# Products of quarters that accumulate in three PSUM banks, in place of seven banks added up by VectorE

## The chip, the cores and the metric

One core of a Trainium2 chip runs the whole program. The metric is the device time of one execution in microseconds; the time of a kernel is the median of its runs. TensorE multiplies and writes PSUM (eight banks); VectorE, ScalarE and GpSimd do the elementwise work, GpSimd on SBUF alone; SyncE issues the DMAs. In the profile they are PE (its weight loads are PEld), DVE, ACT, POOL and SP.

## The reference

64 graphs of 256 nodes with 512 features go through two layers, each on a normalised input (`h = relu(layernorm(x))`) and added to `x`. All values are float32.

```python
# layer 0: graph attention, one head
Wh = h @ W
logits = leaky_relu(Wh @ a_src [rows] + Wh @ a_dst [columns], 0.2)
x = x + softmax(where(adj, logits, -inf)) @ Wh
# layer 1: multi-head attention, 8 heads of 64
q, k, v = h @ Wq.T + bq, h @ Wk.T + bk, h @ Wv.T + bv
scores = where(adj, q @ k.T / sqrt(64), -inf)
x = x + (softmax(scores) @ v) @ Wo.T + bo
```

## The kernel before

**Products of quarters.** A product of a 256 x 512 and a 512 x 512 matrix is taken in quarters: each factor is split two by two, and seven products of quarters (of sums and differences of quarters) replace eight. GpSimd makes the four sums of the left factor (`combine`, L163 to L168), in the order s[0], s[1], s[2], s[3]; the weights' sums are made once. Product 0 uses the left quarter a(0,0), 1 uses s[1], 2 uses a(0,1), 3 uses s[2], 4 uses s[0], 5 uses a(1,1) and 6 uses s[3]. `products` (L170) gives each its own PSUM bank from a pool of eight, and after each product calls `read`, which adds the bank to the quarters of the result that it belongs to.

Four product sets of this kind run per graph. W, in `transform0`, adds the first layer's result to the rows of x; O, in `output`, the second layer's. Both read with `add_to_rows` (L723), one VectorE instruction for each product that adds the bank to as many as four quarters of x at once (`TARGETS`). K, in `project_qk`, makes q and k together (eight matmuls of 128 columns per product, `product_cols`), and V, in `project_v`, makes v. These two read with `add_up` (L190), in which VectorE forms intermediate sums; ScalarE reads product 0 and, in K, copies product 4 with a bias into `p5` for VectorE. A fifth set, U in `aggregate0`, also uses `products` and `add_up`; each of its products has two matmuls.

**The pass.** The program is unrolled in Python, and each engine executes its own queue in the order in which the program issues. That order is written out by hand in two lists: `first_half` (L1072) and `second_half` (L1075). One pass through both handles several graphs at different stages. Each letter runs its stage up to the next `yield`, so each K, V, W or O is one product with its read. In `first_half` the products of O (graph i-2) and K (graph i) alternate; between the first O and the first K stands D0, whose VectorE part is four dot products of 128 x 512 (L526). AS_OLD issues the sums `as` of O's left factor on GpSimd after the first K. O takes its products in the order 0, 2, 5, 1, 3, 4, 6, the other sets in the order 0 to 6. The exponentials of E0 (L557, L558) wait on ScalarE for a DMA.

In `second_half` come A (attention: scores in all eight banks, exponentials on ScalarE, masks on VectorE), the seven W, and among them the first V, then N1, the statistics of the next graph: N1 (`normalize1`, L738) is a mean and a sum of squares on ScalarE for one half of the rows, then, one step later, for the other half, then the normalised rows `xn`. After these come the other six products of V, with A's masks, U, and X1. X1 (`transpose1`, L766) transposes `xn` in two steps; ScalarE writes the result into `hT` (L779), of which there is one buffer, and its third step issues the sums `hs` on GpSimd, also one buffer. `hT` and `hs` are the left factor of the next K and V. The end of the list is X1, V, X1, V, X1, and then the next pass begins with O and K.

Of the kernel before, what the change touches and what calls it, by code (L numbers as in the profile page):

```python
# [9 lines left out]
F32 = mybir.dt.float32  # L10
I32 = mybir.dt.int32
AF = mybir.ActivationFunctionType
# [4 lines left out]
P = 128  # L17
# [11 lines left out]
def kernel(  # L29
# [102 lines left out]
    def bounded():  # L132
# [37 lines left out]
        def products(a, s, name, product, read, order=range(7)):  # L170


            plan = (
                (a(0, 0), B11),
                (s[:, 1], T2),
                (a(0, 1), B21),
                (s[:, 2], T3),
                (s[:, 0], T1),
                (a(1, 1), T4N),
                (s[:, 3], B22),  # L180
            )
            for n in order:
                left, slot = plan[n]
                ps = bank([P, D], f"{name}_{n}")
                product(ps, left, slot)
                read(n, ps)
                yield

        def add_up(n, ps, dst, s2):

            if n == 1:
                nc.vector.tensor_add(s2, dst(0, 0), ps)
            elif n == 2:
                nc.vector.tensor_add(dst(0, 0), dst(0, 0), ps)  # L194
            elif n == 3:
                nc.vector.tensor_add(dst(1, 0), s2, ps)
            elif n == 4:
                nc.vector.tensor_add(dst(1, 1), dst(1, 0), ps)
                nc.vector.tensor_add(dst(0, 1), s2, ps)
            elif n == 5:  # L200
                nc.vector.tensor_add(dst(1, 0), dst(1, 0), ps)
            elif n == 6:
                nc.vector.tensor_add(dst(0, 1), dst(0, 1), ps)

        def product_rows(wt, dst, left, slot):
            for c in range(2):
                nc.tensor.matmul(  # L207
                    dst[:, 0:HD], left[:, c, :], wt[:, slot, c, :], start=c == 0, stop=c == 1
                )

        def product_cols(wts, dst, left, slot):
            for n, wt in enumerate(wts):
                for e in range(2):
                    at = (2 * n + e) * P
                    for c in range(2):
                        nc.tensor.matmul(  # L216
                            dst[:, at : at + P], wt[:, slot, c, e * P : (e + 1) * P], left[:, c, :],
                            start=c == 0, stop=c == 1,
                        )

        xts = {}
# [81 lines left out]

        bias0 = weights.tile([P, 4], F32, tag="bias0", name="bias0")
        bias10 = weights.tile([P, 4], F32, tag="bias10", name="bias10")

        def prepare_biases():
            for n, col in enumerate((cols["bq"], cols["bk"])):  # L310
                nc.vector.tensor_copy(bias0[:, 2 * n : 2 * n + 2], col[:, 0:2])
                nc.vector.tensor_sub(bias10[:, 2 * n : 2 * n + 2], col[:, 2:4], col[:, 0:2])

        def whole(wt):

# [362 lines left out]
        def layer0(g):  # L678
# [37 lines left out]
                if m == 0:  # L716
                    yield

        TARGETS = (
            (0, 4, 1), (1, 4, 1), (0, 1, 1), (2, 4, 1), (1, 4, 2), (2, 3, 1), (1, 2, 1)  # L720
        )

        def add_to_rows(xt, n, ps):  # L723

            quarters = xt.rearrange("p t (j d) -> p (t j) d", j=2)
            first, end, step = TARGETS[n]
            dst = quarters[:, first:end:step, :]
            src = ps[:, 0:HD].unsqueeze(1).to_broadcast([P, dst.shape[1], HD])
            nc.vector.tensor_add(dst, src, dst)  # L729

        def transform0(g):

            a, s = sums0.pop(g)
            yield from products(
                a, s, f"po0_{g}", partial(product_rows, w_sb), partial(add_to_rows, xts[g])
            )

        def normalize1(g):  # L738
            xt = xts[g]

            first = 1 if g else 0
            if g:
                xn = junk = big.tile([P, NT, D], F32, tag="xn", name=f"xn_{g}")
            else:
                junk = work.tile([P, NT, D], F32, tag="ex", name="junk_1", bufs=4)
            stats = Stats(xt, junk, f"1_{g}")
            stats.mean(first)
            stats.squares(first)
            yield
            stats.mean(1 - first)  # L750
            stats.squares(1 - first)
            nmr, rstd = stats.close()
            yield
            if g == 0:
                xn = big.tile([P, NT, D], F32, tag="xn", name=f"xn_{g}")
            for t in range(NT):
                nc.scalar.activation(
                    xn[:, t, :], xt[:, t, :], AF.Identity,
                    bias=nmr[:, t : t + 1], scale=rstd[:, t : t + 1],
                )  # L760
            norms[g] = xn
            yield
# [22 lines left out]
        def project_qk(g):  # L785
            halves = [
                big.tile([P, 4, TOK], F32, tag=f"qk{j}", name=f"qk{j}_{g}")
                for j in range(2)
            ]
            qkv[g] = halves  # L790
            if g == 0:

                for e in range(DC):
                    for n, (wt, nm) in enumerate(((wq_sb, "bq"), (wk_sb, "bk"))):
                        ps = bank([P, TOK], f"pqk_{g}_{e}_{n}")
                        for c in range(DC):
                            part = whole(wt)[c // 2][e // 2][:, c % 2, :]
                            nc.tensor.matmul(
                                ps, part[:, (e % 2) * P : (e % 2 + 1) * P], hT_0[0][:, c, :],
                                start=(c == 0), stop=(c == DC - 1),  # L800
                            )
                        nc.scalar.activation(
                            halves[e // 2][:, 2 * n + e % 2, :], ps, AF.Identity,
                            bias=cols[nm][:, e : e + 1],
                        )
                        yield
                return
            a, s = lefts[g]

            s2 = work.tile([P, 4, P], F32, tag="s2", name=f"s2_{g}")  # L810
            held = []

            def dst(i, j):
                return halves[j][:, :, i * P : (i + 1) * P]

            def read(n, ps):
                ps = ps.rearrange("p (c n) -> p c n", c=4)
                if n == 0:
                    for c in range(4):
                        nc.scalar.activation(  # L820
                            dst(0, 0)[:, c, :], ps[:, c, :], AF.Identity, bias=bias0[:, c : c + 1]
                        )
                elif n == 4:
                    p5 = work.tile([P, 4, P], F32, tag="p5", name=f"p5_{g}")
                    for c in range(4):
                        nc.scalar.activation(
                            p5[:, c, :], ps[:, c, :], AF.Identity, bias=bias10[:, c : c + 1]
                        )
                    held.append(p5)
                    return  # L830
                if held:
                    add_up(4, held.pop(), dst, s2)
                add_up(n, ps, dst, s2)

            yield from products(a, s, f"pqk_{g}", partial(product_cols, (wq_sb, wk_sb)), read)

        def project_v(g):
            a, s = lefts.pop(g)
            v = [big.tile([P, NT, HD], F32, tag=f"v{j}", name=f"v{j}_{g}") for j in range(2)]
            s2 = work.tile([P, HD], F32, tag="s2v", name=f"s2v_{g}")  # L840
            vs[g] = v

            def dst(i, j):
                return v[j][:, i, :]

            def read(n, ps):
                if n == 0:
                    nc.scalar.copy(dst(0, 0), ps[:, 0:HD])
                add_up(n, ps[:, 0:HD], dst, s2)

            yield from products(a, s, f"pv_{g}", partial(product_rows, wv_sb), read)

        def attention(g):

# [137 lines left out]
        def output(g):  # L992
            xt = xts.pop(g)
            a, s = outs.pop(g)
            def store(t):
                row = (g * NT + t) * P
                nc.sync.dma_start(out_rows[row : row + P, :], xt[:, t, :])

            def read(n, ps):
                add_to_rows(xt, n, ps)  # L1000
                if n in (4, 6):
                    store(1 if n == 4 else 0)

            if g < G - 2:

                yield from products(
                    a, s, f"po1_{g}", partial(product_rows, wo_sb), read, (0, 2, 5, 1, 3, 4, 6)
                )
                return

            for t in range(NT):
# [325 lines left out]
```

## Time and profile before

| what | us |
|---|---|
| median of three runs (2813.95 to 2815.35) | 2814.04 |
| span of the profiled execution | 2812.4 |
| one pass of the loop (from one W product to the same one of the next pass) | 43.2 |
| VectorE: add_to_rows (L729), 875 reads | 594.6 |
| VectorE: masks of the attention (L879), 512 | 368.3 |
| VectorE: dot products (L526), 252 | 276.3 |
| VectorE: sums of K from SBUF (L198, L199), 63 each | 84.8 and 75.8 |
| ScalarE: K's product 0 (L820) and product 4 (L826), 252 each | 71.8 and 70.1 |
| ScalarE: exponentials of the attention (L874), 512 | 257.8 |
| GpSimd: longest wait, for a DMA (L606) | 454.1 |

The span is the time from the first to the last instruction of one profiled execution. "Busy" is the time in which an engine had an instruction running; matmuls overlap, so a group's busy time is less than its count times its mean. A matmul of float32 appears as two records. "Idle before" is the time that an engine stood ahead of a group, with the instruction that ended it. GpSimd's and ScalarE's long waits are not by themselves a cost: what counts is who is late for TensorE.

### The profile page before, as it was taken

How to read it: one execution, taken by the hardware profiler on the slowest of the kernel's cores; microseconds unless marked ns; L12 is line 12 of the kernel's file. 1: busy time of each engine (PE TensorE's matmuls, PEld its weight loads, DVE VectorE, ACT ScalarE, POOL GpSimd, SP SyncE). 2: the span in 40 equal slices, each digit the busy share in tenths (PEclk: the TensorE clock that was granted, in tenths of full speed). 3: DMA queues.
4: the chain of work that ended last, by engine and by line, in shares of the span. 5: the costliest groups of instructions: out<-in, count | busy, mean ns of one | idle time of the engine just before them, and what ended most of it. 6: DMA issues, size and time to landing. Idle time of an engine off the chain costs nothing. (4 is left out here: it accounts for less than half of the span.)

```text
span 2812.4 us, 54529 instructions
## 1 busy us (share of the span) xinstructions
PE 2797.5 (99%) x20560; PEld 2462.1 (88%) x20560; DVE 2333.9 (83%) x3942; ACT 1255.3 (45%) x3033; POOL 1505.3 (54%) x2020
## 2 busy tenths in 40 slices
PE   9999999999999999999999999999999999999999
PEld 6888988988889889888898898888988988889886
DVE  7888888888888888888888888888888888888875
ACT  6354453443544444534444445344444453444532
POOL 2745555555555555555555554555555645555541
PEclk9999999999999999999999999999999999999999
DMA  4233343343333434433434344334343443343331
GB/s 135 29 44 41 41 52 37 44 49 40 44 42 41 52 38 44 51 37 44 43 40 52 39 44 52 37 44 44 42 48 39 43 52 37 44 44 42 40 45 28
DMA packets 144321, 127.15 MB, mean 45 GB/s; under 512 B 65204, under 2 KB 110132, under 8 KB 144054
## 3 DMA queue, kind: packets, MB, share of 16 engines
q1 hardware_dynamic: 143958, 123.61, 36.8%
q8 instruction: 165, 2.70, 0.4%
q14 instruction: 102, 0.84, 0.1%
q0 software_dynamic: 96, 0.01, 0.0%
HBM read 41.43 MB, written 33.55 MB: 27 GB/s over the span
## 5 line engine op out<-in xcount | busy, mean ns | idle before, releaser
L729 DVE TENSOR_TENSOR x<-po,x 128x1024 f32<-128x1024 f32 x875 | 594.6, 686 | 149.0 <-PE po L207 141.8
L879 DVE TENSOR_TENSOR ex<-ex,maskT 128x512 f32<-128x512 f32 x512 | 368.3, 760 | 0.0
L606 POOL TENSOR_TENSOR em<-em,rb 128x256 f32<-128x256 f32 x122 | 86.3, 728 | 454.1 <-DMA rb<-rc 454.1
L874 ACT ACTIVATE ex<-psc 128x512 f32<-128x512 f32 x512 | 257.8, 627 | 99.7 <-PE psc L866 99.7
L526 DVE SCALAR_TENSOR_TENSOR junk<-wa,h 128x512 f32<-128x512 f32 x252 | 276.3, 1096 | 7.6 <-ACT h L519 0.9
L216 PEld LDWEIGHTS pqk<-hs,wq_sb 128*128 128x128 f32 x2016 | 264.3, 192 | 13.5 <-POOL hs L166 0.7
L216 PE MATMUL pqk<-hs,wq_sb 128*128 128x128 f32 x2016 | 265.9, 275 | 0.5 <-POOL hs L166 0.5
L216 PE MATMUL pqk<-hs,wk_sb 128*128 128x128 f32 x2016 | 266.3, 275 | 0.0
L557 ACT ACTIVATE e<-es_b,ed 128x256 f32<-128x256 f32 x122 | 61.0, 500 | 445.0 <-DMA es_b<-es_row 445.0
L207 PE MATMUL po<-wo_sb,as 128*128 128x256 f32 x992 | 255.2, 380 | 0.0
L207 PE MATMUL pv<-wv_sb,hs 128*128 128x256 f32 x1024 | 252.6, 379 | 0.5 <-DVE v L194 0.5
L207 PE MATMUL po<-w_sb,us 128*128 128x256 f32 x1008 | 248.4, 379 | 0.0
L216 PEld LDWEIGHTS pqk<-hs,wk_sb 128*128 128x128 f32 x2016 | 245.4, 192 | 0.0
L866 PE MATMUL psc<-qk 64*128 64x256 f32 x2048 | 240.0, 384 | 0.0
L891 PE MATMUL pav<-ex,v 128*64 128x256 f32 x2048 | 237.0, 382 | 1.2 <-DVE ex L879 1.2
L565 POOL TENSOR_TENSOR em<-e,maskT 128x512 f32<-128x512 f32 x62 | 79.6, 1284 | 266.8 <-DVE e L562 257.1
L165 POOL TENSOR_TENSOR hs<-hT 128x256 f32<-128x256 f32 x64 | 47.3, 738 | 320.9 <-PE pv L207 320.9
L866 PEld LDWEIGHTS psc<-qk 64*128 64x128 f32 x2048 | 194.0, 188 | 27.1 <-ACT aT L899 0.8
L207 PEld LDWEIGHTS po<-w_sb,us 128*128 128x128 f32 x1008 | 191.5, 190 | 26.0
L207 PEld LDWEIGHTS pv<-wv_sb,hs 128*128 128x128 f32 x1024 | 189.6, 190 | 24.0 <-DVE v L194 0.9
L899 ACT COPY aT<-pav 128x512 f32<-128x512 f32 x128 | 74.9, 585 | 297.8 <-PE pav L891 130.8
L891 PEld LDWEIGHTS pav<-ex,v 128*64 128x64 f32 x2048 | 141.3, 137 | 75.7 <-DVE ex L879 2.5
(218 smaller groups left out, 6403.5 us busy)
## 6 DMA issues: line engine op xcount, KB each, us to landing
x<-in_x_dram SPq DMA_DIRECT2D x64, 512.0 KB, 5.6
out_dram<-x SPq DMA_DIRECT2D x128, 256.0 KB, 2.0
rb<-rc SPq DMA_DIRECT2D x496, 64.0 KB, 5.1
es_b<-es_row SPq DMA_DIRECT2D x61, 128.0 KB, 6.4
rb<-rc SPq DMA_DIRECT2D x244, 32.0 KB, 3.8
es_row<-es SPq DMA_DIRECT2D x122, 0.5 KB, 1.9
wq_sb<-in_L_gnn_Wq_dram SPq DMA_DIRECT2D x4, 256.0 KB, 8.1
wk_sb<-in_L_gnn_Wk_dram SPq DMA_DIRECT2D x4, 256.0 KB, 6.7
```

The lines of the kernel that those rows point to most:

```text
L207: nc.tensor.matmul(dst[:, 0:HD], left[:, c, :], wt[:, slot, c, :], start=c == 0, stop=c == 1)
L216: nc.tensor.matmul(dst[:, at : at + P], wt[:, slot, c, e * P : (e + 1) * P], left[:, c, :], start=c == 0, stop=c == 1,)
L526: nc.vector.scalar_tensor_tensor(junk, (wa if g else pas)[a], 1.0, h[:, t, :], op0=ALU.mult, op1=ALU.mult, accum_out=dst[:, t : t + 1],)
L557: nc.scalar.activation(e1[:, m, :], pe, AF.Exp, bias=ed[:, m : m + 1])
L565: engine.tensor_tensor(em, e1, maskT, op=ALU.mult)
L606: nc.gpsimd.tensor_tensor(em[:, m, :], em[:, m, :], rb, op=ALU.mult)
L729: nc.vector.tensor_add(dst, src, dst)
L866: nc.tensor.matmul(psc[r][:, m, :], qk[rows, 2 + e % 2, m * P : (m + 1) * P], qk[rows, e % 2, :], start=True, stop=True,)
L874: nc.scalar.activation(ex[:, r, :, :], psc[r], AF.Exp, scale=SCALE)
L879: nc.vector.tensor_mul(ex[:, r, :, :], ex[:, r, :, :], maskT)
L891: nc.tensor.matmul(pav[r * DH : (r + 1) * DH, i, :], v[j][:, m, at : at + DH], pair[i][:, r, m, :], start=(m == 0), stop=(m == NC - 1),)
L899: nc.scalar.copy(aT[j], pav)
```

## The change

W, O, K and V use `chained` in place of `products`. The products run in the order 0, 2, 1, 4, 3, 6, 5 in three banks: 0, 1, 3 and 5 in bank `a`, 2 in `b`, 4 and 6 in `d`. Only the first product in a bank starts it anew; the later ones add to what stands in it. The bank is read after each product, before the next one is written on top, so each read gives one quarter of the result, or one addend of it, and the intermediate sums of VectorE fall away. O loses its own order. ScalarE now copies products 0, 1, 4 and 5 in K (with a bias, four instructions each) and in V (one each); VectorE adds 2, 3 and 6. In W and O VectorE reads every product and adds it to one quarter. `normalize1` takes the rows' first half first, and `output` stores the second half of the rows after product 5 and the first after product 6. U stays as it was.

```diff
+        CHAIN = ((0, "a"), (2, "b"), (1, "a"), (4, "d"), (3, "a"), (6, "d"), (5, "a"))
+        def chained(a, s, name, product, read):
...
+            banks = {}
+            for n, key in CHAIN:
+                left, slot = plan[n]
+                first = key not in banks
+                if first:
+                    banks[key] = bank([P, D], f"{name}_{key}")
+                product(banks[key], left, slot, first)
+                read(n, banks[key])
+                yield
+        def assemble(n, ps, dst, copy):
+            if n == 0:
+                copy(dst(0, 0), ps, 0)
+            elif n == 2:
+                nc.vector.tensor_add(dst(0, 0), dst(0, 0), ps)
+            elif n == 1:
+                copy(dst(0, 1), ps, 1)
+            elif n == 4:
+                copy(dst(1, 1), ps, 1)
+            elif n == 3:
+                nc.vector.tensor_add(dst(1, 1), dst(1, 1), ps)
+            elif n == 6:
+                nc.vector.tensor_add(dst(0, 1), dst(0, 1), ps)
+            elif n == 5:
+                copy(dst(1, 0), ps, 0)
...
-                    dst[:, 0:HD], left[:, c, :], wt[:, slot, c, :], start=c == 0, stop=c == 1
+                    dst[:, 0:HD], left[:, c, :], wt[:, slot, c, :],
+                    start=first and c == 0, stop=c == 1, skip_group_check=not first,
...
-                            start=c == 0, stop=c == 1,
+                            start=first and at == 0 and c == 0, stop=c == 1,
+                            skip_group_check=True,
...
-        bias0 = weights.tile([P, 4], F32, tag="bias0", name="bias0")
-        bias10 = weights.tile([P, 4], F32, tag="bias10", name="bias10")
+        biases = [weights.tile([P, 4], F32, tag=f"bias{j}", name=f"bias{j}") for j in range(2)]
...
-        TARGETS = (
-            (0, 4, 1), (1, 4, 1), (0, 1, 1), (2, 4, 1), (1, 4, 2), (2, 3, 1), (1, 2, 1)
-        )
+        TARGETS = ((0, 0), (0, 1), (0, 0), (1, 1), (1, 1), (1, 0), (0, 1))
...
-            nc.vector.tensor_add(dst, src, dst)
+            t, j = TARGETS[n]
+            part = xt[:, t, j * HD : (j + 1) * HD]
+            nc.vector.tensor_add(part, ps[:, 0:HD], part)
...
-            yield from products(
+            yield from chained(
                 a, s, f"po0_{g}", partial(product_rows, w_sb), partial(add_to_rows, xts[g])
...
-            first = 1 if g else 0
+            first = 0
...
+            def copy(to, ps, j):
+                for c in range(4):
+                    nc.scalar.activation(
+                        to[:, c, :], ps[:, c, :], AF.Identity, bias=biases[j][:, c : c + 1]
+                    )
...
-            yield from products(a, s, f"pqk_{g}", partial(product_cols, (wq_sb, wk_sb)), read)
+                assemble(n, ps.rearrange("p (c n) -> p c n", c=4), dst, copy)
+            yield from chained(a, s, f"pqk_{g}", partial(product_cols, (wq_sb, wk_sb)), read)
...
+            def copy(to, ps, j):
+                nc.scalar.copy(to, ps)
...
-            yield from products(a, s, f"pv_{g}", partial(product_rows, wv_sb), read)
+                assemble(n, ps[:, 0:HD], dst, copy)
+            yield from chained(a, s, f"pv_{g}", partial(product_rows, wv_sb), read)
...
-                if n in (4, 6):
-                    store(1 if n == 4 else 0)
+                if n in (5, 6):
+                    store(1 if n == 5 else 0)
...
-                yield from products(
-                    a, s, f"po1_{g}", partial(product_rows, wo_sb), read, (0, 2, 5, 1, 3, 4, 6)
-                )
+                yield from chained(a, s, f"po1_{g}", partial(product_rows, wo_sb), read)
```

More of the change, by code (lines that the diff above doesn't have):

```diff
@@ L187, in products @@
                 yield
+        CHAIN = ((0, "a"), (2, "b"), (1, "a"), (4, "d"), (3, "a"), (6, "d"), (5, "a"))
+        def chained(a, s, name, product, read):
+            plan = (
+                (a(0, 0), B11),
+                (s[:, 1], T2),
+                (a(0, 1), B21),
+                (s[:, 2], T3),
+                (s[:, 0], T1),
+                (a(1, 1), T4N),
+                (s[:, 3], B22),
+            )
[23 more added lines that the diff above has]
+                copy(dst(1, 0), ps, 0)
         def add_up(n, ps, dst, s2):
@@ L203, in add_up, with product_rows, product_cols @@
                 nc.vector.tensor_add(dst(0, 1), dst(0, 1), ps)
-        def product_rows(wt, dst, left, slot):
+        def product_rows(wt, dst, left, slot, first):
             for c in range(2):
                 nc.tensor.matmul(
-                    dst[:, 0:HD], left[:, c, :], wt[:, slot, c, :], start=c == 0, stop=c == 1
+                    dst[:, 0:HD], left[:, c, :], wt[:, slot, c, :],
+                    start=first and c == 0, stop=c == 1, skip_group_check=not first,
                 )
-        def product_cols(wts, dst, left, slot):
+        def product_cols(wts, dst, left, slot, first):
             for n, wt in enumerate(wts):
@@ L302, in busy @@
                 nc.tensor.transpose(scratch, ident, ident)
-        bias0 = weights.tile([P, 4], F32, tag="bias0", name="bias0")
-        bias10 = weights.tile([P, 4], F32, tag="bias10", name="bias10")
+        biases = [weights.tile([P, 4], F32, tag=f"bias{j}", name=f"bias{j}") for j in range(2)]
         def prepare_biases():
             for n, col in enumerate((cols["bq"], cols["bk"])):
-                nc.vector.tensor_copy(bias0[:, 2 * n : 2 * n + 2], col[:, 0:2])
-                nc.vector.tensor_sub(bias10[:, 2 * n : 2 * n + 2], col[:, 2:4], col[:, 0:2])
+                for j in range(2):
+                    nc.vector.tensor_copy(
+                        biases[j][:, 2 * n : 2 * n + 2], col[:, 2 * j : 2 * j + 2]
+                    )
         def whole(wt):
@@ L717, in layer0 @@
                     yield
-        TARGETS = (
-            (0, 4, 1), (1, 4, 1), (0, 1, 1), (2, 4, 1), (1, 4, 2), (2, 3, 1), (1, 2, 1)
-        )
+        TARGETS = ((0, 0), (0, 1), (0, 0), (1, 1), (1, 1), (1, 0), (0, 1))
         def add_to_rows(xt, n, ps):
[L725 to L729, printed above, removed]
+            t, j = TARGETS[n]
+            part = xt[:, t, j * HD : (j + 1) * HD]
+            nc.vector.tensor_add(part, ps[:, 0:HD], part)
         def transform0(g):
             a, s = sums0.pop(g)
-            yield from products(
+            yield from chained(
                 a, s, f"po0_{g}", partial(product_rows, w_sb), partial(add_to_rows, xts[g])
@@ L808, in project_qk @@
             a, s = lefts[g]
-            s2 = work.tile([P, 4, P], F32, tag="s2", name=f"s2_{g}")
-            held = []
             def dst(i, j):
                 return halves[j][:, :, i * P : (i + 1) * P]
-            def read(n, ps):
[L817 to L821, printed above, removed]
-                        )
[L823 to L833, printed above, removed]
-            yield from products(a, s, f"pqk_{g}", partial(product_cols, (wq_sb, wk_sb)), read)
+            def copy(to, ps, j):
+                for c in range(4):
+                    nc.scalar.activation(
+                        to[:, c, :], ps[:, c, :], AF.Identity, bias=biases[j][:, c : c + 1]
+                    )
+            def read(n, ps):
+                assemble(n, ps.rearrange("p (c n) -> p c n", c=4), dst, copy)
+            yield from chained(a, s, f"pqk_{g}", partial(product_cols, (wq_sb, wk_sb)), read)
         def project_v(g):
@@ L839, in project_v @@
             v = [big.tile([P, NT, HD], F32, tag=f"v{j}", name=f"v{j}_{g}") for j in range(2)]
-            s2 = work.tile([P, HD], F32, tag="s2v", name=f"s2v_{g}")
             vs[g] = v
@@ L844, in dst @@
                 return v[j][:, i, :]
+            def copy(to, ps, j):
+                nc.scalar.copy(to, ps)
             def read(n, ps):
-                if n == 0:
-                    nc.scalar.copy(dst(0, 0), ps[:, 0:HD])
-                add_up(n, ps[:, 0:HD], dst, s2)
-            yield from products(a, s, f"pv_{g}", partial(product_rows, wv_sb), read)
+                assemble(n, ps[:, 0:HD], dst, copy)
+            yield from chained(a, s, f"pv_{g}", partial(product_rows, wv_sb), read)
         def attention(g):
@@ L1000, in read @@
                 add_to_rows(xt, n, ps)
-                if n in (4, 6):
-                    store(1 if n == 4 else 0)
+                if n in (5, 6):
+                    store(1 if n == 5 else 0)
             if g < G - 2:
-                yield from products(
-                    a, s, f"po1_{g}", partial(product_rows, wo_sb), read, (0, 2, 5, 1, 3, 4, 6)
-                )
+                yield from chained(a, s, f"po1_{g}", partial(product_rows, wo_sb), read)
                 return
```

## The prediction

> **What bounds the kernel now.** I read the page first, then the table of waits, then one pass of the loop (1400 to 1445 us) engine by engine in order of time. On the page:
>
> ```profile
> PE 2797.5 (99%) x20560; PEld 2462.1 (88%) x20560; DVE 2333.9 (83%) x3942; ACT 1255.3 (45%) x3033; POOL 1505.3 (54%) x2020
> ```
>
> TensorE is busy for 99% of the span. The same product of W starts at 1402.30 and at 1445.51, so a pass takes 43.21 us, nearly all of it back-to-back matmuls. Two-matmul products follow each other 0.864 us apart (four records of 216 ns), those of K take 1.785 us. The table of waits says who is late for whom; TensorE's own waits come to about 11 us in the whole span.
>
> ```profile
> POOL hs L165 <- PE pv L207: 320.9, 63, 5.5
> ACT hT L779 <- PE pv L207: 118.0, 63, 2.5
> ACT xn L472 <- DVE x L729: 82.3, 63, 2.7
> ```
>
> The reader is to see that other engines wait for TensorE, that V's products hold up the next hT on ScalarE and the next hs on GpSimd in every pass, and that the norm's statistics start when VectorE has read W's last needed product. So nothing taken off VectorE shortens the loop. Only a new wait of TensorE changes it. The positions that matter, on TensorE:
>
> ```profile
> 1404.03 1.03 PE L207 MATMUL po<-w_sb,uT 128*128 128x256 f32 x4
> 1407.48 1.89 PE L207 MATMUL pv<-wv_sb,hs 128*128 128x256 f32 x8
> 1412.77 1.03 PE L207 MATMUL pv<-wv_sb,hT 128*128 128x256 f32 x4
> 1414.07 1.03 PE L207 MATMUL pv<-wv_sb,hs 128*128 128x256 f32 x4
> 1414.94 1.03 PE L207 MATMUL po<-wo_sb,aT 128*128 128x256 f32 x4
> 1420.23 1.03 PE L207 MATMUL po<-wo_sb,aT 128*128 128x256 f32 x4
> 1422.88 1.03 PE L207 MATMUL po<-wo_sb,as 128*128 128x256 f32 x4
> ```
>
> The sixth W product starts at 1404.03, the fourth and fifth V at 1407.48 and 1408.34, the sixth and seventh V at 1412.77 and 1414.07, the first, third and fourth O at 1414.94, 1420.23 and 1422.88. The first sum `as` is used by the fourth O. On ScalarE, GpSimd and VectorE in the same pass:
>
> ```profile
> 1405.59 0.63 ACT L472 ACTIVATE xn<-x 128x512 f32<-128x512 f32 x1 [1.30 <-DVE x L729]
> 1408.53 1.51 ACT L519 ACTIVATE h<-x,nmr,rstd 128x512 f32<-128x512 f32 x2
> 1413.84 1.08 ACT L779 ACTIVATE hT<-pt 128x512 f32<-128x512 f32 x2 [1.88 <-PE pv L207]
> ```
> ```profile
> 1417.43 0.73 POOL L168 TENSOR_TENSOR hs<-hT,hs 128x256 f32<-128x256 f32 x1
> 1418.11 1.18 POOL L165 TENSOR_TENSOR as<-aT,aT 128x256 f32<-128x256 f32 x1
> 1419.37 1.05 POOL L166 TENSOR_TENSOR as<-as,aT 128x256 f32<-128x256 f32 x1
> 1417.54 1.17 DVE L526 SCALAR_TENSOR_TENSOR junk<-wa,h 128x512 f32<-128x512 f32 x1
> ```
>
> The statistics of the norm hold ScalarE from 1405.59 to 1408.53 (2.94 us). The new hT is written from 1413.84, 0.04 us after the product at 1412.77 ends: that is V's product 5, the last reader of the old hT. A GpSimd sum that starts before VectorE's dot products takes 0.73 us, one that starts during them 1.05 to 1.18.
>
> **What the Trainium skill says.** "SBUF — State Buffer", section "Who interferes with whom": a VectorE operation with two inputs in SBUF and a GpSimd operation exclude each other, whichever starts later waits. The lines above agree, and VectorE's reads from PSUM don't slow GpSimd (`us`, 0.73 us). "TensorE: Matmul & The Clock Gate", section "What's actually happening": after an idle window of about 3.4 us the clock halves for a window. This trace is stricter: a 2.10 us wait is enough (93 to 95 us; busy 1.31 of 3.41 us, then a window at half clock):
>
> ```profile
> 92.46:95.87 3.41, 1.31 (x24) 0.70 (x18) 3.38 (x6) 0.15 (x1) 3.25 (x4) 1.00 0.01 2
> 95.87:99.28 3.41, 3.41 (x18) 2.77 (x16) 3.41 (x4) 1.69 (x4) 3.41 (x4) 0.50 0.20 15
> ```
>
> "PSUM — Partial Sum Buffer", section "PSUM bank collisions raise a hardware error": a matmul may not write a bank while another engine reads it, so each product in a shared bank waits for the read before it. The trace of before, with a bank per product, shows no such wait in the loop.
>
> **The change part by part.** *VectorE and ScalarE.* A product set of W or O read by VectorE took 1.219 + 0.957 + 2 x 0.689 + 3 x 0.416 = 4.80 us; seven reads of 0.416 are 2.91. K loses five reads of 0.672 and two SBUF sums of 1.346 and 1.204, and keeps or gains three of 0.672: minus 3.9. V goes from seven of 0.412 to three: minus 1.65. That is 9.3 us per pass off VectorE, about 580 us of its 2334. ScalarE gains eight small copies in K (two groups of 1.14 us) and three of 0.373 in V, 3.4 us per pass. TensorE was not waiting for VectorE, so the saving is worth nothing; the additions cost by where they stand. Biases and start flags: nothing measurable, the biases once and hidden in the start.
>
> *Waits between neighbours in W* (1 after 0, 6 after 4, 5 after 3: one product between). From the start of a product: its last matmul ends at 1.03, VectorE starts 0.04 later, reads for 0.416, and TensorE's first matmul is effective 0.16 after a release (0.055 to the weight load's start, then the load's 0.10, as where it waited for hs at 74.8 us). Sum 1.64 against 1.73: hidden, with 0.09 us to spare. Behind other VectorE work it would cost that delay; none stands there. O and K have more than a product of K between such pairs: hidden.
>
> *V's product 3 waits for ScalarE's copy of product 1.* The new order has V 2, 1, 4, 3. The copy of 1 stands in ScalarE's queue behind both halves of the statistics, which now start after W's product 6 in the sixth place. From that product's start: end and read 1.48, ScalarE starts 0.04 later, statistics 2.94, copy 0.373, to TensorE 0.16: 4.99. Product 3 would be due at 5 x 0.864 = 4.32. TensorE stands for 0.67 us, and with it the queue behind it: U, X1, O. 63 passes: 42 us.
>
> *hT is held by V's last product.* Product 5 reads hT itself and moves from the sixth to the seventh place (1412.77 to 1414.07), after both transposes. The new hT can be written only after it: ScalarE starts 1.07 after product 5's start, needs 1.08 for two halves, and GpSimd starts the sums `hs` 0.09 later, at 2.24. Before, `hs` started at 1415.25, 1.18 on the same scale. K's first product needs the first half: 1.07 + 0.595 + 0.16 = 1.82 against 1.73, which is 0.09 late and part of what follows.
>
> *O's product 1 moves from the fourth to the third place* and needs the second `as` sum, sixth in GpSimd's queue. The dot products (L526) start at 0.864 + 1.07 + 0.33 = 2.26, since O's first read is now 0.416 and not 1.22, and run 4.57 to 6.83. First `hs` 2.24; the next three and the first `as` each start during a dot product: second 3.05, third 4.07, fourth 5.20, `as` 6.34, second `as` 7.59, this one free at 0.73: 8.32, and 8.48 with the way to TensorE. If the dot product wins the tie at 2.24, the slow ones are the first four and the end is the same within 0.1 to 0.4. Product 1 would be due at O + K + O + K behind product 5, 0.864 + 2 x 0.864 + 2 x 1.785 = 6.16. So 2.32 us per pass, with the 0.09 in it. 60 passes have the dot products beside them: 139 us; two more about 0.6 each; the two ends of the program about 2.
>
> *The clock.* Of the 2.32 us some 2.22 are one stretch, against 2.10 that halved the clock. With free windows of 3.41 us, (3.41 - 2.22 + 2 x 0.11)/3.41 = 41% of passes have such a window; if half-busy is enough, 65%. A window at half clock loses at most 1.7 us. I take 27 windows at 1.6: 43 us. Below nothing this can't go; the upper end is 60 x 1.7 = 102.
>
> Sum on the profiled execution: 2812.4 + 42 + 139 + 3 + 43 = 3039; the median of the runs, 2814.04, is 1.6 above its span: 3041, taken as 3040.
>
> **The rivals.** *The clock holds*: the same waits, no half windows: 2998. For it: one case only in the trace before, and my 2.22 is near it. *hT isn't held*: the halves are released apart or the wait ends earlier, so `hs` starts at 0.88 on the scale above; four sums are slowed all the same and O's product 1 is 0.9 late, no clock windows: 2812 + 42 + 56 + 3 = about 2914. Against it: the 118.0 us of ScalarE's waits for V. *More of it*: half windows in nearly every pass, or X1's first transpose also late for a bank that VectorE still reads (0.15 us to spare in my sum): 3110 to 3130. *On the other side*: the queues don't hold program order, so that V's copy and the `as` sums overtake what they stand behind. All loop waits vanish, and with 9 us less on VectorE the waits of the first pass (3.3 us on masks and edge sums near 88 to 95 us, plus 1.7 of half clock) go: 2808. It decides only if both late spots, 0.67 and 2.32, fall under zero. Against it: ScalarE stands 7.13 us before the exponentials of weights0 with K's copies queued behind.
>
> **How the numbers follow.** Forecast 0.42 (2990 to 3090 of its own); clock holds 0.24; hT not held 0.18; more 0.11; other side 0.05, of which 0.02 faster by over 0.2% and 0.03 within. 0.2% is about what a measurement of this kernel can tell from no change. The range 2905 to 3100 takes in the bounds of the clock and the hT case. Slower has 0.95.
>
> **What would show it.** Waits of TensorE: V (L207) for ScalarE's copy of pv about 0.6 us, 63 times; O (L207) for GpSimd L166 about 2.2 us, 60 times; ScalarE's hT starting behind V's last product; `hs` sums at 1.1 us; clock below 0.99; VectorE near 1750 us. I am wrong if the pass stays under 44 us, or if TensorE's longest waits name VectorE.

## The result, and the profile after

| kernel | median us | runs | from, to |
|---|---|---|---|
| before | 2814.33 | 4 | 2813.95 to 2815.35 |
| after | 3078.03 | 4 | 3076.97 to 3079.77 |

The ratio is 1.0937, with a 95% interval of 1.0922 to 1.0953: the change makes the kernel 9.4% slower. The profiled execution has a span of 3076.2 us, 263.8 more than before. The line of busy times on the page of after:

```profile
PE 2915.8 (95%) x20560; PEld 2532.1 (82%) x20560; DVE 1773.5 (58%) x3434; ACT 1443.4 (47%) x3729; POOL 1486.3 (48%) x2020
```

VectorE has lost 560 us of work (about 580 were reckoned), and TensorE has the same 20560 matmul records, but it now stands for 160 us of the span instead of 15. And its own busy time has grown by 118 us with the same work: most of that is work at half clock (some 80 us, as counted below), the rest about 0.3 us that each of the 124 waits in the first two lines of the next table adds to the modelled busy time. The table of waits of after (engine, line, what it waited for: us in all, times, longest):

```profile
POOL hs L165 <- ACT hT L818: 402.2, 63, 7.3
...
ACT hT L818 <- PE pv_a L247: 214.7, 63, 4.2
...
PE po_a L247 <- POOL as L166: 115.3, 62, 2.3
...
PE pv_a L247 <- ACT v L872: 23.9, 62, 0.6
...
PE pqk_a L257 <- DVE qk L223: 7.4, 1, 7.4
```

Three waits of TensorE are new: O's product 1 waits for the second sum `as` on GpSimd, V's product 3 for ScalarE's copy of product 1, and, once, a product of K for VectorE. The first two come in every pass. TensorE in one pass, in order of time (start, duration, and in brackets the idle time before):

```profile
1534.76 1.03 PE L247 MATMUL pv_d<-wv_sb,hs 128*128 128x256 f32 x4
1536.16 1.13 PE L247 MATMUL pv_a<-wv_sb,hs 128*128 128x256 f32 x4 [0.38 <-ACT v L872]
1537.13 0.61 PE L677 MATMUL pu<-em,h 128*128 128x128 f32 x4
...
1539.81 0.70 PE L677 MATMUL pu<-em,hq 128*128 128x128 f32 x4
1540.35 0.60 PE L817 MATMUL pt<-ident,xn 128*128 128x128 f32 x4
...
1542.09 1.03 PE L247 MATMUL pv_a<-wv_sb,hT 128*128 128x256 f32 x4
1542.95 1.03 PE L247 MATMUL po_a<-wo_sb,aT 128*128 128x256 f32 x4
1543.81 1.14 PE L257 MATMUL pqk_a<-hT,wq_sb 128*128 128x128 f32 x8
1544.80 1.06 PE L257 MATMUL pqk_a<-hT,wk_sb 128*128 128x128 f32 x8
1545.69 1.03 PE L247 MATMUL po_b<-wo_sb,aT 128*128 128x256 f32 x4
...
1550.43 1.13 PE L247 MATMUL po_a<-wo_sb,as 128*128 128x256 f32 x4 [1.93 <-POOL as L166]
```

V's product 3 should follow its neighbour after 0.864 us, at 1535.62. U, which follows it, starts at 1537.13, where 1536.49 was due: 0.64 us lost. The bracket shows less, 0.38, because a matmul's modelled end lies 0.17 after its slot (1.03 against 0.864) and the product then takes 1.13 in place of 1.03, with the new weights to be loaded first. U's last product (1539.81) takes 0.54 to X1 where it took 0.45 before: 0.09 late. K's first product takes 0.99 to its second half instead of 0.89: 0.10 late. The last line is O's product 1, with 1.93 us of idle time before it. ScalarE, GpSimd and VectorE explain these spots:

```profile
1532.83 0.63 ACT L515 ACTIVATE xn<-x 128x512 f32<-128x512 f32 x1 [1.26 <-DVE x L768]
...
1535.76 0.35 ACT L872 COPY v<-pv_a 128x256 f32<-128x256 f32 x1
...
1539.40 0.35 ACT L688 COPY uT<-pu 128x256 f32<-128x256 f32 x1
...
1543.15 1.08 ACT L818 ACTIVATE hT<-pt 128x512 f32<-128x512 f32 x2 [3.41 <-PE pv_a L247]
```
```profile
1544.31 0.72 POOL L165 TENSOR_TENSOR hs<-hT 128x256 f32<-128x256 f32 x1 [6.38 <-ACT hT L818]
1545.12 1.06 POOL L166 TENSOR_TENSOR hs<-hs,hT 128x256 f32<-128x256 f32 x1
1546.14 1.17 POOL L167 TENSOR_TENSOR hs<-hT 128x256 f32<-128x256 f32 x1
1547.27 1.17 POOL L168 TENSOR_TENSOR hs<-hT,hs 128x256 f32<-128x256 f32 x1
1548.40 1.17 POOL L165 TENSOR_TENSOR as<-aT,aT 128x256 f32<-128x256 f32 x1
1549.65 0.72 POOL L166 TENSOR_TENSOR as<-as,aT 128x256 f32<-128x256 f32 x1
```
```profile
1544.36 1.23 DVE L569 SCALAR_TENSOR_TENSOR junk<-wa,h 128x512 f32<-128x512 f32 x1
```

The copy of V's product 1 starts 2.93 us after the statistics, because it is queued behind them. ScalarE's copy of U's product 0, further back in the same queue, ends at 1539.75, and the weights of U's last product begin to load 0.05 us later, here as in all 61 passes with such a product; presumably the two products share a bank, which the trace doesn't show. hT is written 1.06 us after the start of V's last product (1542.09), which still reads the old hT. The first `hs` starts just ahead of VectorE's dot products and takes 0.72; the next four start beneath them and take 1.06 to 1.17. The second `as`, which O's product 1 needs, starts behind them and takes 0.72 again.

The pass has two lengths: 46.23 us, 3.02 more than before, and 47.86. The difference is the clock. Columns of the next lines: the window, its length, then busy us and instruction count of TensorE, its weight loads, VectorE, ScalarE and GpSimd, granted clock, share of the DMA engines, GB/s.

```profile
1406.72:1410.14 3.42, 1.49 (x14) 1.30 (x13) 2.85 (x6) 0.00 (x0) 3.34 (x5) 1.00 0.02 0
1410.14:1413.55 3.41, 3.41 (x12) 3.05 (x13) 0.42 (x1) 0.00 (x0) 3.33 (x6) 0.50 0.68 24
...
1502.30:1505.71 3.41, 1.51 (x9) 1.41 (x10) 1.75 (x5) 0.00 (x0) 3.33 (x5) 1.00 0.24 9
1505.71:1509.13 3.42, 3.42 (x29) 3.32 (x28) 0.51 (x2) 1.14 (x4) 3.34 (x5) 1.00 0.79 25
```

After a window with 1.49 us of work and the whole wait inside, the next window runs at half clock (0.50). After a window with 1.51 us of work, where the wait had begun 0.02 us ahead of it, it doesn't. Of the 57 passes between the start and the end 46 contain such a window, each 1.64 us longer. So 57 x 3.02 + 46 x 1.64 = 248 us; the remaining 16 us lie before the first product of attention and values (10), in the three passes after it (3), and in the last two passes and the end (3).

### The profile page after: what moved, and what is told of

It is laid out like the page before. It is cut to its first block, busy times and chain, and to the rows that moved or that the text cites. A ratio compares the mean times of both kernels' runs of the same rounds, so it can differ in the third digit from the quotient of the medians.

```text
span 3076.2 us, 54206 instructions
## 1 busy us (share of the span) xinstructions
PE 2915.8 (95%) x20560; PEld 2532.1 (82%) x20560; DVE 1773.5 (58%) x3434; ACT 1443.4 (47%) x3729; POOL 1486.3 (48%) x2020
## 5 line engine op out<-in xcount | busy, mean ns | idle before, releaser
L854 ACT ACTIVATE qk<-pqk_a,bias 128x128 f32<-128x128 f32 x756 | 215.5, 368 | 882.6 <-PE pqk_a L257 882.6
L768 DVE TENSOR_TENSOR x<-po_a,x 128x256 f32<-128x256 f32 x500 | 212.4, 425 | 376.4 <-PE po_a L247 372.4
L768 DVE TENSOR_TENSOR x<-po_d,x 128x256 f32<-128x256 f32 x250 | 105.9, 423 | 307.2 <-PE po_d L247 307.2
L247 PE MATMUL po_a<-wo_sb,as 128*128 128x256 f32 x496 | 149.1, 428 | 115.3 <-POOL as L166 115.3
L247 PEld LDWEIGHTS po_a<-wo_sb,as 128*128 128x128 f32 x496 | 89.5, 200 | 134.8 <-POOL as L166 127.0
L907 DVE TENSOR_TENSOR sm<-ex 128x512 f32<-128x512 f32 x256 | 177.9, 695 | 8.9
L257 PEld LDWEIGHTS pqk_a<-hs,wq_sb 128*128 128x128 f32 x1008 | 168.9, 238 | 9.8
L257 PE MATMUL pqk_a<-hs,wq_sb 128*128 128x128 f32 x1008 | 170.3, 325 | 0.0
L995 POOL TENSOR_TENSOR x<-x,bo_b 128x512 f32<-128x512 f32 x128 | 161.5, 1283 | 0.0
L247 PE MATMUL pv_a<-wv_sb,hs 128*128 128x256 f32 x512 | 138.1, 392 | 24.4 <-ACT v L872 23.9
```

Of the source, the lines that this page charges most:

```text
L247: nc.tensor.matmul(dst[:, 0:HD], left[:, c, :], wt[:, slot, c, :], start=first and c == 0, stop=c == 1, skip_group_check=not first,)
L257: nc.tensor.matmul(dst[:, at : at + P], wt[:, slot, c, e * P : (e + 1) * P], left[:, c, :], start=first and at == 0 and c == 0, stop=c == ...
L768: nc.vector.tensor_add(part, ps[:, 0:HD], part)
L854: nc.scalar.activation(to[:, c, :], ps[:, c, :], AF.Identity, bias=biases[j][:, c : c + 1])
L907: nc.vector.tensor_add(sm, ex[:, :, 0, :], ex[:, :, 1, :])
L995: nc.gpsimd.tensor_tensor(part, part, bo_b, op=ALU.add)
```

## The experiments

The theory is that of the prediction: two places where a queue's order makes TensorE wait, the first drawn out by hT's late release and by VectorE holding GpSimd up, and half-clock windows as their consequence. The rival is that sharing a bank is itself what costs: that the products wait for the reads between them or run slower when they accumulate. Further questions were how the two places depend on each other, and what decides on the number of half-clock windows. Each kernel keeps the whole computation. All but the first three start from the kernel after.

**W and K alone.** V and O as before the change; the code is put together from both kernels, with both forms of a function side by side where both are used.

> W and K accumulate in three banks, V and O are as before the change (whole computation kept). Theory: every read of W has 0.09 us to spare, K's reads have microseconds, nothing else of TensorE moves: the pass stays 43.2 us, 2814 us, perhaps 8 us more where the first passes wait for VectorE's masks. Rival that a product in a shared bank costs by its own wait (0.1 to 0.2 us for each of three in W): 2835 us or more.

Measured: 2818.61 us (20 runs; before 2814.46), ratio 1.0014, interval 1.0008 to 1.0021. The pass is 43.20 us and TensorE has no wait in the loop. Its longest wait:

```profile
PE pqk_a L257 <- DVE qk L223: 8.2, 1, 8.2
```

This single wait stands in pass 1, where no O lies between the products of K, and where VectorE has the first graph's masks ahead of K's read. Two of the four product sets thus accumulate in three banks for nothing in the loop; the rival is out for them. W's 0.09 us to spare holds. The 4 us that this kernel is slower lie outside the loop.

**V alone**, and **O alone**.

> V alone accumulates in three banks (whole computation kept). Theory: V's product 3 is 0.64 us late, X1 0.1, K's first product 0.1; O's product 1 is still its fourth, so the later hs sums cost nothing: pass 44.0 us, 2862 us, no half-clock windows. If the wait of V and the wait of O are independent costs, the same.

Measured: 2868.19 us, ratio 1.019 (1.017 to 1.0211), pass 44.05 us. The wait of V's product 3 is there (24.3 us in 62 places), and the table of waits has no other that comes in each pass.

> O alone accumulates in three banks, with its product 1 third (whole computation kept). Theory: hs starts early as before, O's product 1 waits 1.25 us: pass 44.5 us, 2889 us, clock whole. Together with v_only that is 2.1 us of the 3.0 of the whole change: the rest and the half-clock windows come only where V's late release of hT meets O's new order. Rival that O's order costs the same 2.2 us alone: 2950 us without, 3020 us with half-clock windows.

Measured: 2891.34 us, ratio 1.0272 (1.0252 to 1.0293), pass 44.5 us. Its wait in the loop:

```profile
PE po_a L247 <- POOL as L166: 60.2, 60, 1.1
```

V alone costs 0.84 us per pass and O alone 1.34. Together that is 2.2, the whole change costs 3.0 and then the clock. The wait of O grows from 1.07 to 1.92 us only where V keeps hT to its last product.

**V's product 5 ahead of product 6.** The only edit is the order in V:

```diff
-            for n, key in CHAIN:
+            for n, key in order:
...
+        V_CHAIN = CHAIN[0:5] + (CHAIN[6], CHAIN[5])
...
-            yield from chained(a, s, f"pv_{g}", partial(product_rows, wv_sb), read)
+            yield from chained(a, s, f"pv_{g}", partial(product_rows, wv_sb), read, V_CHAIN)
```

> V takes its product 5 before its product 6, nothing else (whole computation kept). Theory: hT is released one product of V earlier, hs starts at 1.18 instead of 2.24 us behind the sixth V product, O's product 1 waits 1.25 us instead of 2.2, K's first product isn't late, and the clock stays whole: pass 45.2 us, 2937 us. If hT's release doesn't matter: 3078. If the half-clock windows stay as many (46) in spite of the shorter wait: 3010.

Measured: 2941.24 us, ratio 1.045 (1.0419 to 1.048), pass 45.2 us. Its waits in the loop:

```profile
PE po_a L249 <- POOL as L166: 58.7, 60, 1.0
PE pv_a L249 <- ACT v L874: 24.0, 62, 0.6
```

Exchanging two neighbours in one list wins back 137 us of 264: 1.0 us of each pass, and with it all 46 half-clock windows of the loop, since no wait is long enough now (O's is 1.0 us).

**The sums `as` ahead of `hs`.**

```diff
-            (load, 3), O, D0, K, AS_OLD, O, K, O, K, O, K, E0, O, US, BO, A_OLD, K, E0, O, K, O, K,
+            (load, 3), O, D0, K, O, K, O, K, O, K, E0, O, US, BO, A_OLD, K, E0, O, K, O, K,
...
-            U0, X1, V, X1, V, X1,
+            U0, X1, V, X1, V, AS, X1,
```

> The sums as of O's left factor are issued ahead of hs on GpSimd (whole computation kept). Theory (TensorE waits for as behind hs): the wait of O's product 1 (2.2 us per pass) goes, K's first product stays 0.1 late, V's product 3 stays 0.64 late, and no half-clock windows are left in the loop, since no stretch is over 2 us: pass 44.0 us, 2868 us in all. Rival (accumulating in a shared bank slows TensorE itself, or the reads of VectorE do): pass stays above 45.5 us, 2960 us or more.

Measured: 2871.08 us, ratio 1.02 (1.0171 to 1.023), pass 44.0 us, clock 0.999. The wait for `as` is gone from the table of waits; V's is unchanged (24.0 us, 62).

**The dot products later.** D0 stands behind O's product 1.

```diff
-            (load, 3), O, D0, K, AS_OLD, O, K, O, K, O, K, E0, O, US, BO, A_OLD, K, E0, O, K, O, K,
+            (load, 3), O, K, AS_OLD, O, K, O, D0, K, O, K, E0, O, US, BO, A_OLD, K, E0, O, K, O, K,
```

> The four dot products D0 of VectorE stand after O's product 1 instead of ahead of it (whole computation kept). Theory (VectorE's two-input reads hold GpSimd's sums up): hs and as run at 0.73 us each, O's product 1 waits 0.4 to 0.5 us instead of 1.9, no half-clock windows; but es_b is asked for 6 us later, and TensorE then waits about 0.8 us per pass for the edge sums (psm). Pass 44.6 to 45.4 us, 2905 to 2950 us. Rival (the sums are late by their place in the queue alone): O's wait stays above 1.5 us and the time above 3000 us.

Measured: 2914.1 us, ratio 1.0355 (1.0336 to 1.0374), pass mostly 44.7 us. GpSimd in this kernel:

```profile
1511.61 0.72 POOL L165 TENSOR_TENSOR hs<-hT 128x256 f32<-128x256 f32 x1 [6.38 <-ACT hT L818]
1512.41 0.73 POOL L166 TENSOR_TENSOR hs<-hs,hT 128x256 f32<-128x256 f32 x1
1513.09 0.73 POOL L167 TENSOR_TENSOR hs<-hT 128x256 f32<-128x256 f32 x1
1513.78 0.73 POOL L168 TENSOR_TENSOR hs<-hT,hs 128x256 f32<-128x256 f32 x1
1514.47 0.73 POOL L165 TENSOR_TENSOR as<-aT,aT 128x256 f32<-128x256 f32 x1
1515.27 0.72 POOL L166 TENSOR_TENSOR as<-as,aT 128x256 f32<-128x256 f32 x1
```

With nothing of VectorE's dot products beside them the six sums take 4.4 us in place of 6.1, and O's wait falls to a median of 0.25 us, less than the 0.4 to 0.5 expected. The feared wait for the edge sums came only now and then (2.6 us in four places).

**U's first products ahead of V's product 3.**

```diff
-            ... A, V, V, V, A, N0, N1, V, U0, AS,
+            ... A, V, V, V, A, U0, N0, N1, V, AS,
```

> The first four products of U are issued ahead of V's product 3 (whole computation kept). Theory: V's product 3 finds ScalarE's copy of product 1 ready, its wait of 0.64 us goes, and X1's 0.1 us for a bank too: pass 45.5 us without a half-clock window. The clock part: a pass with a half-clock window is then 47.1 us, no longer 14 windows of 3.413 us, so the windows come in about 40% of passes instead of 46 of 62: 2995 us. If the number of half-clock windows doesn't hang on the length of the pass: 3033 us.

Measured: 3012.93 us, ratio 1.0704 (1.0673 to 1.0735). The wait of V is gone, and the passes are 45.49 and 47.13 us long, 0.73 less each: V's 0.64 and the 0.09 of U's last product. Half-clock windows: 34 of 56 passes (those with the full wait of 1.9 us), fewer than 46, but 61% and not the expected 40%. The time lies between the two expectations.

**More work for TensorE in each pass.**

```diff
+        def pad(g):
+            busy(4)
+            yield
...
-            todo = first_half + second_half
+            todo = first_half + ([(pad, 0)] if i > 1 else []) + second_half
```

> Four transposes of the identity into an unused bank are added to TensorE at the end of first_half in passes 2 on, about 0.9 us of work per pass; the result is not touched. Theory that the pass locks onto 14 clock windows (47.86 against 47.79 us): with 0.9 us more the lock is off, half-clock windows come in about 23 passes instead of 46, 39 us are won back of the 56 added: 3095 us. Rival that each long wait halves the clock with a fixed chance of 3 in 4: 3134 us.

Measured: 3095.63 us, ratio 1.0998 (1.0966 to 1.103). The time is the expected one, for another reason: the four transposes are one record each and took 0.45 us per pass, half of what I put, and half-clock windows came in 38 of 56 passes, not 23. So the expectation of neither side was right, and the passes of the three kernels were laid against the 3.413 us grid on which their half-clock windows start. That gives a plain rule: a pass gets one when all of the 1.92 us wait falls into one window, which is so if it begins in about the first 0.43 of a window. Wait by wait this is right for 165 of the 168 full waits of the three kernels; the other three lie within 0.03 us of a window's edge. What the next pass meets depends on how many windows the pass was long, with or without the half clock. From nothing but these lengths a pass after the other can be followed, for any start (mean over starts, 60 passes):

```
kernel    pass without, with   in windows        followed     counted
after      46.23   47.86 us    13.54   14.02     51 of 60     46 of 56
pad        46.67   48.31 us    13.67   14.15     40 of 60     38 of 56
u_first    45.49   47.13 us    13.33   13.81     38 of 60     34 of 56
```

The passes of after that get a half-clock window are 14.02 windows long, so the next one starts its wait in the same part of a window, for up to 17 passes in a row. The other two kernels drift faster but are thrown back into the zone by their short passes. The rule was read from these three traces and not tried on a further kernel.

**All three edits together**, and then **with start and end mended**: the masks of the first graph are spread over passes 0 and 1, its bias rows are added later, and V's last graph keeps the order of after.

```diff
-                todo = first + [A, W, N0, E0] + second_half[7:17] + [(sums_of(wq_sb), 0)]
+                todo = first + [A, W, N0, E0] + second_half[7:17] + [A, (sums_of(wq_sb), 0)]
...
-                if i == 1 and n in (4, 9):
+                if i == 1 and n == 16:
                     step(attention, 0)
-                if i == 1 and n == 13:
+                if i == 1 and n == 34:
                     step(bias_rows, 0)
```

> The whole change with all three edits: V's product 5 before 6, U's first products ahead of V's product 3, as ahead of hs (whole computation kept). Theory: no wait of TensorE is left in the loop, the pass is 43.2 us as before; about 7 us more in the first passes: 2820 us. Not faster than before, since TensorE's own work is unchanged. If a part of the 3.0 us per pass has another cause, the pass stays above 43.5 us and the time above 2835 us.

Measured: 2820.61 us (17 runs; before 2814.46), ratio 1.0022 (1.0014 to 1.0029), pass 43.20 us. With all four sets in three banks and no wait in the loop, sharing a bank costs nothing by itself here. The 6 us left lie ahead of the loop (3.4), where TensorE waits 7.8 us for K's read in pass 1, and behind its last product of W (2.2).

> all3 with the start and end mended: masks of the first graph spread over pass 0 and behind K's product 3 in pass 1, the first graph's bias rows later, V's last graph in the other order (whole computation kept). Theory: the loop is as fast as before (43.2 us), and TensorE's 7.8 us wait and the half-clock windows of pass 1 go: 2808 to 2813 us against 2814.3 before. If VectorE is still late for K in pass 1: 2818.

Measured: 2814.41 us (13 runs; before 2814.12), ratio 0.9999 (0.9991 to 1.0007). TensorE's long wait in pass 1 is gone, two shorter ones for the edge sums and for a read of W (1.4 and 1.2 us) stand in the same pass. The expected gain over the kernel before (2808 to 2813 us) did not come. All that the change costs can be put back by order alone, and the 560 us that it takes off VectorE are then worth nothing measurable.

## Why the prediction was right

The direction and the two places were right, and the two large terms of a pass to a few hundredths. The time lies inside the range, 38 us above the forecast of 3040: 32 more came from the clock and 13 more from the ends of the program, and 9 less from the waits (57 x 3.02 = 172 us against 42 + 139).

- *TensorE bounds the loop, and work taken off VectorE is worth nothing.* Shown by the last experiment: 43.20 us per pass with 9.2 us less on VectorE (27.1 busy us per pass in place of 36.3).
- *Waits between neighbours in W hidden.* Shown by W and K alone. The 0.09 us to spare were enough in every pass.
- *V's product 3, 0.67 us.* Measured 0.64, and shown as the cause by moving U in front of it.
- *hT held by V's last product; `hs` at 2.24 on the prediction's scale.* Measured 1544.31 - 1542.09 = 2.22. Shown by exchanging products 5 and 6.
- *O's product 1, 2.32 us with K's 0.09.* It starts at 1550.43 with 0.10 more to load its weights, so 8.44 behind V's last product at 1542.09, against the 8.48 of the sum. Which sums would be slow (three `hs`, one `as`) came out too. That order, hT and the dot products make this wait together is shown by three experiments that each take one away. The Trainium skill's page "SBUF — State Buffer", section "Who interferes with whom", says that the two share a pair of ports as an exclusive lock and that the order of issue decides which of them is blocked; the 1.06 to 1.17 us against 0.73, and their absence once the dot products are moved, agree.
- *U's last product: a term that the prediction did not have.* It is 0.09 us late in each pass behind ScalarE's copy of U's product 0, and makes up the 3.02. The expectations above call it X1's wait for a bank. The rival of that name (X1's first transpose late for a bank that VectorE still reads) is not what the trace shows: the lateness lies ahead of X1, and ScalarE ends it.
- *The clock: a mis-sized term, and in part luck.* The cost of a window, at most 1.7, was 1.64. The number was wrong: 27 were put, 46 in full passes were found, 75 us in place of 43. The prediction took the 41% of window positions as a chance for each pass, as if every pass fell on the windows anew. But a pass keeps its place in the grid from one to the next, and 47.86 us is 14.02 windows. The luck: the 2.22 us were counted from slot to slot, the 2.10 that they were set against is the idle time that the profile shows. Counted like that the new wait is 1.92 us, shorter than the one case known, so the trace of before could not show that it would be enough.
- *The two ends, 2 us: mis-sized too*, 16 were found. K's product 5 in pass 1 waits 7.4 us for product 3's read, which is queued on VectorE behind three sets of masks. The prediction looked for waits between neighbours in the steady pass only; in pass 1 no O lies between K's products. One sign of being wrong thus came true by the letter: TensorE's longest single wait names VectorE. It comes once; the waits of the loop, 115.3 and 23.9 us in all, name GpSimd and ScalarE.

## What to carry to other kernels

A bank that is read between its products turns a queue's backlog on the reading engine into a wait of TensorE, so before banks are saved, each read's place in its queue has to be compared with the product that will want its bank next. A new order of products moves two more things than the reads: when the first user of each operand comes, and when the last reader lets a single buffer go. Where TensorE was never waiting, work taken from another engine is worth nothing, while every wait put in costs its length, and the clock on top if it is long (1.92 us were enough here, 1.07 were not).

## What the runs showed of the hardware that was not expected

- How sharp the clock's threshold is. In the three kernels with the long wait there are 168 waits of 1.92 to 1.94 us. All 118 that lay inside one window of 3.413 us with 0.04 us or more to its edges were followed by a window at half clock. None of the 47 with 1.91 us or less in any one window was, nor were the three that lay inside but within 0.03 us of an edge. 1.92 of 3.413 us idle is 44% busy. In the trace of after the grid of half-clock windows is the same over 3 ms within 2 ns. The Trainium skill's page "TensorE: Matmul & The Clock Gate", section "HAM oscillation — how this bites in real kernels", names idle gaps over about 3.4 us as the limit; here 1.92 us, less than two thirds of that, is enough.
- That a loop can lock onto this grid. A half-clock window lengthens the pass by 1.64 us, to 14.02 windows, and so brings the next pass's wait to the same place.
